# Conv-attention and a four-block Mamba on one core: group norm's matmuls, statistics loads, input order and the last fusion rescheduled

## The chip, the core and the metric

The kernel runs on one core of a Trainium2 chip. A core has five engines that run side by side, each working through its own queue in order: TensorE (PE in the profile, its weight loads PEld), VectorE (DVE), ScalarE (ACT), GpSimd (POOL) and SyncE (SP), which here only issues DMAs. The metric is the device time of one execution in microseconds (us). Before the change it is 8983.23 us, the median of three runs (8980.16 to 8992.36).

## The reference

The input is x, of shape 8 x 512 x 48 x 48 in fp32: 8 samples of 512 channels and 2304 positions. Two layers follow each other, each with a group norm in front and a residual around it.

```python
x = x + _L0_conv_ref(_gn(x), L0_conv_Wq, ...)    # causal linear attention
x = x + _L1_conv_ref(_gn(x), L1_conv_in_proj_w, ...)
```

Layer 0 projects to q, k and v (8 heads of 64), applies elu + 1 to q and k, and computes causal linear attention over the positions: a running sum of k times v, read by q and divided by q times the running sum of k.

Layer 1 splits the channels into 4 blocks of 128. Block i takes its own channels plus the fused output of block i - 1, and runs a Mamba over the positions: an input projection, a causal convolution of 4 taps, silu, a projection to dt, B and C, softplus, a state recurrence of 16 states for each of 256 inner channels, a gate and an output projection. Then it fuses:

```python
fused_global = jnp.maximum(x_i, x_m)
w_local = jax.nn.sigmoid(jnp.mean(x_i, axis=(2, 3), keepdims=True))
w_global = jax.nn.sigmoid(jnp.mean(fused_global, axis=(2, 3), keepdims=True))
return w_local * x_i + w_global * fused_global
```

The group norm has 32 groups of 16 channels and takes mean and variance over a group's channels and all positions.

## The kernel before

Positions are cut into 6 chunks of 384 (LC). The recurrence is the bulk of the work: a job is one chunk of one block of one sample, 192 jobs in all, each of 8 slots. A slot does four scans on VectorE (`scan`, L844), each with a decay factor from ScalarE's exp into a PSUM bank (`decay`, L833), the product of B and the input partly on VectorE (`product`, L823) and partly on GpSimd (`last_product`, L812), a product with C on GpSimd (`weigh`, L860), and a gather on TensorE that adds the states up (`gather`, L867). Two streams of jobs (even samples, odd samples) alternate by a fixed pattern; the last job is stream 1's.

All other work is written as generators ("tasks") that a planner steps at two places in each slot, `beside(2k)` before the scans of slot k and `beside(2k + 1)` after two of them. These are called halves. A generator yields when its next stage is due and how many PSUM banks the stage needs: a tuple `(half, gap)` means not before that half and at least `gap` halves after its last stage; a string such as `"1"` means that many halves after its last stage. A stage whose banks are not spare is put off, and so are stages behind it that need banks. There are 6 such banks; three usually hold decays. The engines run what is issued in the order of issue, so the planner's order is every queue's order.

The tasks are these. `chunk(m)` is one attention chunk for one block of 128 channels; its stages are due at `times[m] + j`, and its end copies the new x from PSUM (L463), takes statistics of it (bn_stats, L467), and after the sixth chunk runs `group_norm` for that block's input of layer 1. `group_norm` (L162) has five stages, whose places its caller can give: aggregate the statistics and a first matmul that averages over groups (L171), subtract (L174 to L178), a second matmul (L186), add epsilon and a power on GpSimd (L188, L191), and the factors (L195). `statistics(b)` takes the statistics of a whole sample for layer 0's group norm: for samples above 0 it loads 24 pieces, one each 16 halves (`PERIOD`), and runs bn_stats on each (L239); for sample 0 it loads x in six large DMAs (L219). `weights()` loads a block's weights for a stream (L493 to L510) and scales the convolution's on GpSimd (L516). `pass_on()` fuses the block that has ended and writes the input of the next one, `xi`, chunk by chunk: ScalarE scales the maximum `fu` and `xi` (L610, L611), GpSimd adds them (L618), and the new `xi` is either the sum with the normalized x (L623, blocks 1 to 3), or, when a new sample starts (`fresh`), the normalized x alone, written by ScalarE (L621); it may overwrite `xi` only after the add at L618 has read it. GpSimd then adds the residual (L626), and the result is stored. `self.ready` tells the planner that a job may begin. `prepare()` of a job makes its convolution (L649) and the rest, due at fixed halves ahead of the job's first slot. Its softplus writes `delta` (L720) and frees two banks late.

`save` and `flush` put off stores by a few halves; SP issues loads and stores in the planner's order.

Of the kernel before, what the change touches and what calls it, by code (L numbers as in the profile page):

```python
# [9 lines left out]
F32 = mybir.dt.float32  # L10
AF = mybir.ActivationFunctionType
ALU = mybir.AluOpType
# [4 lines left out]
P = 128  # L17
T = 128
LC = 384
# [30 lines left out]
def attention_then_mamba_kernel(  # L50
# [17 lines left out]
    nc = tc.nc  # L68
    B, _, L = x.shape
    NS = 16  # L70
    NC = L // LC
# [5 lines left out]
    mpool = ctx.enter_context(tc.tile_pool(name="mamba", bufs=2))  # L77
# [21 lines left out]
    def load_projections(o):  # L99

        src = wqkv.rearrange("(t p) c -> p t c", p=P)
        for j in range(3):
            cols = slice(j * 512 + o * P, j * 512 + (o + 1) * P)
            nc.sync.dma_start(out=wq_sb[:, :, cols], in_=src[:, :, cols])
# [49 lines left out]
    def save(out, in_):  # L154
        stores.append((half_no[0], out, in_))

    def flush(every=True):
        while stores and (every or stores[0][0] <= half_no[0] - 2):
            _, o, i = stores.pop(0)
            nc.sync.dma_start(out=o, in_=i)  # L160
# [46 lines left out]
    norms, xns, x1s, done, ksums = {}, {}, {}, {}, {}  # L207

    def statistics(b):

        xv = x[b].rearrange("(t p) l -> p t l", p=P)
        stats = small.tile([P, 4, NC, 6], F32, tag="stats_a", name=f"stats_a{b}", bufs=2)
        if b == 0:

            xs = []

            def load(c):
                t = mpool.tile([P, 4, 1 + LC], F32, tag="u", name=f"xs_{c}", bufs=5)[:, :, 0:LC]
                nc.sync.dma_start(out=t, in_=xv[:, :, c * LC : (c + 1) * LC])  # L219
                xs.append(t)  # L220

            for c in range(5):
                load(c)
            load_projections(0)
            for c in range(NC):
                for ct in range(4):
                    nc.vector.bn_stats(stats[:, ct, c, :], xs[c][:, ct, :])
                if c == 0:
                    load(5)
                    fetch(0)  # L230
            for o in range(1, 4):
                load_projections(o)
        else:
            when = begins[b] + b % 2
            for i in range(4 * NC):
                yield (when - 2, 1) if b > 1 else "1", 0
                xs = piece(b, i)
                yield (when, 1) if b > 1 else "1", 0
                nc.vector.bn_stats(stats[:, i // NC, i % NC, :], xs)  # L239
                when += PERIOD  # L240
        norms[b] = yield from group_norm(stats, 4, f"a{b}", 2)

    def piece(b, i):
        ct, c = i // NC, i % NC
        xs = apool.tile([P, LC], F32, tag="xs", name=f"xs_{b}_{i}", bufs=2)
        nc.sync.dma_start(out=xs, in_=x[b][ct * P : (ct + 1) * P, c * LC : (c + 1) * LC])
        return xs
# [3 lines left out]
    def fetch(m):  # L251

        if m == len(parts):
            return
        b, o, c = parts[m]
        if (o, c) == (0, 0):
            xns[b] = dpool.tile([512, L], F32, tag="xn", name=f"xn_{b}", bufs=B)
            x1s[b] = dpool.tile([512, L], F32, tag="x1", name=f"x1_{b}", bufs=B)
        xn = apool.tile([P, 4, LC], F32, tag="xn", name=f"xn_{b}_{o}_{c}", bufs=2)
        src = (x[b] if o == 0 else xns[b]).rearrange("(t p) l -> p t l", p=P)  # L260
        nc.sync.dma_start(out=xn, in_=src[:, :, c * LC : (c + 1) * LC])
        fetched[m] = xn
# [3 lines left out]
    def chunk(m):  # L266


        b, o, c = parts[m]
# [3 lines left out]
        cols, tile_rows = slice(c * LC, (c + 1) * LC), slice(o * P, (o + 1) * P)  # L273
# [58 lines left out]
        S, stats, ksum = passes[b, o]  # L332
# [107 lines left out]
        for i in range(NT):  # L440
            old = c > 0 or i > 0
# [25 lines left out]
        nc.vector.bn_stats(stats[:, 0, c, :], xr)  # L467
        if c + 1 == NC:
            norm = yield from group_norm(
                stats, 1, f"m{b}_{o}", 8, [(times[m] + j, 1) for j in (28, 29, 29, 30, 32)]  # L470
            )
            flush()
            done[b, o] = norm

    class Stream:
# [62 lines left out]
        def pass_on(self):  # L538


            xi = self.xi
            old = None
            if self.b is not None:
                old = self.b, self.s, self.n, self.fm
                wt = small.tile([P, 4], F32, tag="wt", name=f"wt_{self.n}")
                nc.vector.tensor_copy(wt[:, 2:3], self.sums)
                nc.vector.tensor_reduce(wt[:, 3:4], self.fsum, AX.X, ALU.add)
            last = old is not None and old[1] == 3 and not self.samples
# [29 lines left out]
            def loads(c):  # L578
                fu = xb = xa = None
                cols = slice(c * LC, (c + 1) * LC)  # L580
                if not last:
                    xb = mpool.tile([P, LC], F32, tag="xb", name=f"xb_{self.n}_{c}")
                    nc.sync.dma_start(out=xb, in_=x1s[self.b][s * P : (s + 1) * P, cols])
                if old is not None:
                    fu = mpool.tile([P, LC], F32, tag="fu", name=f"fu_{old[2]}_{c}")
                    nc.sync.dma_start(out=fu, in_=old[3][:, cols])
                    xa = mpool.tile([P, LC], F32, tag="xo", name=f"xo_{old[2]}_{c}")
                    nc.sync.dma_start(out=xa, in_=x1s[old[0]][old[1] * P : (old[1] + 1) * P, cols])
                return fu, xb, xa

            now = loads(0)
            for c in range(NC):

                if c and not last:
                    first = 2 * self.jobs[self.block * NC + c].start
                    yield (first - 33, 1), 0
                    now = loads(c)
                    yield (first - 25, 1), 0
                elif c:
                    yield "3", 0  # L600
                    now = loads(c)
                    yield "1", 0
                else:
                    yield "1", 0
                cols, icols = slice(c * LC, (c + 1) * LC), slice(3 + c * LC, 3 + (c + 1) * LC)
                fu, xb, xa = now
                if not last:
                    normed = dict(bias=norm[:, 1, :], scale=norm[:, 0, :])
                if old is not None:
                    nc.scalar.activation(fu, fu, AF.Copy, scale=wt[:, 1:2])  # L610
                    nc.scalar.activation(xi[:, icols], xi[:, icols], AF.Copy, scale=wt[:, 0:1])  # L611
                if old is None:
                    nc.scalar.activation(xi[:, icols], xb, AF.Identity, **normed)
                elif not last and not self.fresh:
                    nc.scalar.activation(xb, xb, AF.Identity, **normed)
                if old is not None:
                    yield "1", 0
                    nc.gpsimd.tensor_tensor(fu, fu, xi[:, icols], ALU.add)  # L618
                    yield "1", 0
                    if not last and self.fresh:  # L620
                        nc.scalar.activation(xi[:, icols], xb, AF.Identity, **normed)  # L621
                    elif not last:
                        nc.gpsimd.tensor_tensor(xi[:, icols], xb, fu, ALU.add)  # L623
                    self.ready = c + 1
                    yield "1", 0
                    nc.gpsimd.tensor_tensor(xa, xa, fu, ALU.add)  # L626
                    save(out[old[0], old[1] * P : (old[1] + 1) * P, cols], xa)
                self.ready = c + 1
# [331 lines left out]
    def first_scan(b, o):  # L960
        own = [j.start for j in jobs if j.stream is streams[b % 2]]
        return own[(b // 2 * 4 + o) * NC]

    parts, times = [], []
    for b, o in sorted(((b, o) for b in range(B) for o in range(4)), key=lambda t: first_scan(*t)):
        for c in range(NC):
            when = 2 * first_scan(b, o) - BEFORE - (NC - 1 - c) * PERIOD
# [75 lines left out]
    def at(k):  # L1043
        return jobs[k // SLOTS], k % SLOTS
# [31 lines left out]
    def prime(k):  # L1076
        job, s = at(k)
        hurry(k, lambda: job.prepared)
        primed.add(k)
        job.inputs(0)  # L1080
        for r in range(2):
            us[k + r] = job.last_product(s + r)
        job.product(s, us[k])
        ahead(DEPTH)
# [48 lines left out]

    with tc.manual_schedule():
        half_no[0] = FIRST - 6
        for st in streams:
            tasks.append(Task(st.weights()))
            tasks.append(Task(st.pass_on()))
        Task(statistics(0)).finish()
        for half in range(FIRST - 6, 0):  # L1140
            beside(half)
        prime(0)
        for k in range(slots):
            slot(k)
# [70 lines left out]
```

## Time and profile before

| | us |
|---|---|
| median of three runs | 8983.23 |
| profiled execution | 8983.06 |
| its span (first to last instruction) | 8981.0 |
| VectorE busy in it | 8252.1 |
| GpSimd busy | 8058.8 |
| TensorE busy | 7759.3 |
| ScalarE busy | 6629.5 |

The profile is of one execution. Its span is divided into busy and idle time for each engine; for idle time it names what ended it, the instruction or DMA whose completion the engine waited for. Busy TensorE time is modelled, as matmuls are pipelined. The five costliest groups of instructions (line, engine, operation, shapes and count | busy us, mean ns of one | idle time of the engine just before them, and what ended it):

```profile
L844 DVE TENSOR_TENSOR_SCAN u<-bank,u 128x385 f32<-128x385 f32 (+1 forms) x6144 | 5449.4, 937 | 273.8 <-ACT bank L833 253.5
L860 POOL TENSOR_TENSOR u<-u,C 128x1536 f32<-128x1536 f32 x1536 | 4880.9, 3178 | 142.8 <-DVE u L844 36.1
L833 ACT ACTIVATE bank<-dr,av 128x385 f32<-128x385 f32 (+1 forms) x6144 | 3418.0, 578 | 995.0 <-DVE u L844 768.6
L867 PE MATMUL yp<-u,cst 128*64 128x384 f32 x12288 | 2471.0, 524 | 389.7 <-POOL u L860 313.1
L812 POOL TENSOR_TENSOR u<-B,dxr 128x512 f32<-128x512 f32 x1536 | 1958.9, 1275 | 19.6 <-DMA dxr<-xscr 17.5
```

### The profile page before, as it was taken

What the parts mean: (1) busy time and instruction counts of PE and PEld (TensorE: products, weight loads), DVE (VectorE), ACT (ScalarE), POOL (GpSimd) and SP (SyncE); (2) the same over time, 40 slices, a digit from 0 to 9 for tenths busy, and PEclk for the clock granted to TensorE, in tenths of its full rate; (3) what the DMA queues carried; (4) which work ended last, traced back from release to release, by engine and by line L of the source; (5) the groups of instructions that cost most, each with busy time, mean ns of one, the idle gap of its engine ahead of it and who ended that gap; (6) DMA issues with size and microseconds to landing.
All of it is one profiled execution on the core that took longest, in us unless ns stands there. A gap on an engine that the chain in (4) does not pass through costs nothing.

```text
span 8981.0 us, 121595 instructions
## 1 busy us (share of the span) xinstructions
PE 7759.3 (86%) x36098; PEld 3681.5 (41%) x36098; DVE 8252.1 (92%) x11448; ACT 6629.5 (74%) x12848; POOL 8058.8 (90%) x5635
## 2 busy tenths in 40 slices
PE   7888888888888889888888888898888888888864
PEld 4444444443444444443344444444444444444321
DVE  3999999998899999999999999999989999999997
ACT  2777777777777777777777777777777777777775
POOL 1888999999999899999998999998999999999998
PEclk9999999999999999999999999999999999999987
DMA  6666776666666677676666667676666676666654
GB/s 189 163 176 180 192 190 189 187 186 186 188 181 180 182 192 193 188 185 189 188 187 184 182 187 191 191 192 182 189 188 187 182 187 181 182 181 179 173 156 131
DMA packets 1002901, 1642.89 MB, mean 183 GB/s; under 512 B 138593, under 2 KB 797313, under 8 KB 1002241
## 3 DMA queue, kind: packets, MB, share of 16 engines
q1 hardware_dynamic: 1002240, 1635.13, 67.2%
q8 instruction: 287, 4.70, 0.2%
q14 instruction: 374, 3.06, 0.1%
HBM read 1309.06 MB, written 325.58 MB: 182 GB/s over the span
## 4 chain that ended last, share of the span: by engine, by line
DVE 37%; POOL 13%; PE 13%; ACT 13%; DMA 11%; issue 8%; SPq 4%; POOLq 0%; DVEq 0%; ACTq 0%
DVE u L844 23%; POOL u L860 8%; DVE u L823 7%; ACT bank L833 4%; PE bank L286 4%; PE yp L867 3%; SPq L753 3%; PE bank L649 3%; DMA C<-scr 2%; POOL u L812 2%; ACT L833 2%; ACT L720 2%; DMA dscr<-delta 1%; DVE yz L879 1%; DMA xo<-x 1%
## 5 line engine op out<-in xcount | busy, mean ns | idle before, releaser
L844 DVE TENSOR_TENSOR_SCAN u<-bank,u 128x385 f32<-128x385 f32 (+1 forms) x6144 | 5449.4, 937 | 273.8 <-ACT bank L833 253.5
L860 POOL TENSOR_TENSOR u<-u,C 128x1536 f32<-128x1536 f32 x1536 | 4880.9, 3178 | 142.8 <-DVE u L844 36.1
L833 ACT ACTIVATE bank<-dr,av 128x385 f32<-128x385 f32 (+1 forms) x6144 | 3418.0, 578 | 995.0 <-DVE u L844 768.6
L867 PE MATMUL yp<-u,cst 128*64 128x384 f32 x12288 | 2471.0, 524 | 389.7 <-POOL u L860 313.1
L812 POOL TENSOR_TENSOR u<-B,dxr 128x512 f32<-128x512 f32 x1536 | 1958.9, 1275 | 19.6 <-DMA dxr<-xscr 17.5
L823 DVE TENSOR_TENSOR u<-B,dxp 128x1024 f32<-128x1024 f32 x1536 | 1833.1, 1193 | 10.6 <-ACT dxp L796 10.6
L286 PE MATMUL bank<-xn,wq_sb 128*128 128x384 f32 x4608 | 1681.1, 508 | 88.3 <-POOL xn L310 33.2
L867 PEld LDWEIGHTS yp<-u,cst 128*64 128x64 f32 x12288 | 788.5, 141 | 1615.6 <-issue 865.7
L649 PE MATMUL bank<-xi,wk 128*128 128x384 f32 x3072 | 1104.1, 502 | 274.3 <-ACT kl L383 184.1
L286 PEld LDWEIGHTS bank<-xn,wq_sb 128*128 128x128 f32 x4608 | 854.1, 196 | 833.9 <-DVE k L351 137.7
L649 PEld LDWEIGHTS bank<-xi,wk 128*128 128x128 f32 x3072 | 556.0, 191 | 834.0 <-ACT kl L383 290.8
L298 ACT ACTIVATE ex<-bank,bqkv_sb 128x384 f32<-128x384 f32 x384 | 221.3, 576 | 639.3 <-PE bank L286 639.2
L761 POOL TENSOR_TENSOR delta<-delta,xs 128x384 f32<-128x384 f32 x384 | 384.3, 1001 | 255.8 <-DMA dscr<-delta 191.0
L858 POOL COPY state<-u 128x4 f32<-128x4 f32 x1280 | 242.0, 189 | 334.9 <-DVE u L844 329.0
L833 ACT ACT_TABLE_LOAD x382 | 490.1, 1283 | 6.8
L801 ACT ACTIVATE yp<-xs,pv 128x384 f32<-128x384 f32 x384 | 223.9, 583 | 316.7 <-DVE yz L879 316.5
L709 PE MATMUL bank<-dbc,wd 9*128 9x384 f32 x768 | 316.9, 534 | 1.3 <-ACT dbc L701 1.3
L885 PE MATMUL bank<-yz,wo 128*128 128x384 f32 x768 | 295.6, 506 | 16.3 <-DVE yz L879 14.2
L660 PE MATMUL bank<-xi,wi 128*128 128x384 f32 x768 | 287.4, 496 | 13.1 <-ACT xs L685 13.1
L696 PE MATMUL bank<-xs,wx 128*40 128x384 f32 x768 | 281.0, 488 | 0.8 <-DVE sm L434 0.8
L453 PE MATMUL bank<-sm,v 128*64 128x128 f32 x2304 | 257.6, 302 | 0.0
L416 PE MATMUL bank<-cst,rdb 128*128 128x128 f32 x576 | 120.1, 325 | 150.7 <-DVE u L844 148.7
(111 smaller groups left out, 7902.5 us busy)
## 6 DMA issues: line engine op xcount, KB each, us to landing
B<-scr SPq DMA_DIRECT2D x1536, 192.0 KB
C<-scr SPq DMA_DIRECT2D x1536, 192.0 KB
xn<-xn SPq DMA_DIRECT2D x192, 768.0 KB
dr<-dscr SPq DMA_DIRECT2D x768, 192.0 KB
dxr<-xscr SPq DMA_DIRECT2D x768, 192.0 KB
dscr<-delta SPq DMA_DIRECT2D x192, 384.0 KB
xscr<-delta SPq DMA_DIRECT2D x192, 384.0 KB
xn<-in_x SPq DMA_DIRECT2D x48, 768.0 KB
```

The lines of the kernel that those rows point to most:

```text
L286: nc.tensor.matmul(ps, wq_sb[:, kt, j * 512 + o * P : j * 512 + (o + 1) * P], xn[:, kt, :], start=(kt == 0), stop=(kt == 3),)
L649: nc.tensor.matmul(xc, wk[:, k, h * P : (h + 1) * P], xi[:, c0 + k : c0 + k + LC], start=(k == 0), stop=(k == 3),)
L660: nc.tensor.matmul(zp, wi[:, 256 + h * P : 256 + (h + 1) * P], xi[:, c0 + 3 : c0 + 3 + LC], start=True, stop=True,)
L709: nc.tensor.matmul(vp, wd[32:41, h * P : (h + 1) * P], dbc[32:41, :], start=True, stop=True)
L761: nc.gpsimd.tensor_tensor(delta[:, h, :], delta[:, h, :], xs[:, h, :], ALU.mult)
L812: nc.gpsimd.tensor_tensor(u[:, :, :, 1 + LC - TAIL :], self.B[s % 4][:, :, cols].unsqueeze(2).to_broadcast(shape), self.dxr[s // 4][:, :, ...
L823: nc.vector.tensor_mul(u[:, :, :, 1 : 1 + LC - TAIL], self.B[s % 4][:, :, cols].unsqueeze(2).to_broadcast(shape), self.dxp.unsqueeze(1).to ...
L833: nc.scalar.activation(dA[:, cols], self.dr[h][:, g, cols], AF.Exp, scale=self.w[6][:, 2 * h + g, q + j : q + j + 1],)
L844: nc.vector.tensor_tensor_scan(u[:, j, g, cols], dA[:, cols], u[:, j, g, cols], 0.0, ALU.mult, ALU.add,)
L860: nc.gpsimd.tensor_tensor(h, h, self.C[s % 4].unsqueeze(2).to_broadcast([P, NG, 2, LC]), ALU.mult)
L867: nc.tensor.matmul(self.yp[g * 64 : g * 64 + 64, 0:LC], pair_sum, u[:, j, g, 1:], start=False, stop=(s % 4 == 3 and j == NG - 1), skip_gro ...
L885: nc.tensor.matmul(self.xm[:, 0:LC], self.w[2][:, h, :], self.yz[:, h, :], start=(h == 0), stop=(h == 1),)
```

## The change

Five edits. The group norm of layer 1 gets new places: its first stage with the bn_stats in front of it, its second matmul with the subtraction. A sample's statistics pieces are loaded four halves before their bn_stats rather than two. A fresh input chunk after the first is written two halves after the add rather than one. Sample 0's statistics, with their loads, are issued before the weights and streams are set up. And the last fusion of stream 1, which has no block after it, is written anew: it loads everything at once into three of the large `u` buffers and does the two multiply-adds of each chunk on VectorE.

```diff
             for i in range(4 * NC):
-                yield (when - 2, 1) if b > 1 else "1", 0
+                yield (when - 4, 1) if b > 1 else "1", 0
                 xs = piece(b, i)
...
             norm = yield from group_norm(
-                stats, 1, f"m{b}_{o}", 8, [(times[m] + j, 1) for j in (28, 29, 29, 30, 32)]
+                stats, 1, f"m{b}_{o}", 8, [at(28, 0), at(29), at(29, 0), at(30), at(32)]
             )
...
+            if last and self.z:
+
+                got = [
+                    mpool.tile([P, 4, 1 + LC], F32, tag="u", name=f"end_{i}", bufs=5)
+                    for i in range(NC // 2)
+                ]
+                for c in range(NC):
+                    fu, xa = (got[c // 2][:, c % 2 * 2 + i, 0:LC] for i in range(2))
+                    cols = slice(c * LC, (c + 1) * LC)
+                    rows = slice(old[1] * P, (old[1] + 1) * P)
+                    nc.sync.dma_start(out=xa, in_=x1s[old[0]][rows, cols])
+                    nc.sync.dma_start(out=fu, in_=old[3][:, cols])
+                for c in range(NC):
+                    fu, xa = (got[c // 2][:, c % 2 * 2 + i, 0:LC] for i in range(2))
+                    cols, icols = slice(c * LC, (c + 1) * LC), slice(3 + c * LC, 3 + (c + 1) * LC)
+                    for t, i in ((xi[:, icols], 0), (fu, 1)):
+                        nc.vector.scalar_tensor_tensor(
+                            xa, t, wt[:, i : i + 1], xa, ALU.mult, ALU.add
+                        )
+                    nc.sync.dma_start(out=out[old[0], rows, cols], in_=xa)
+                return
             now = loads(0)
...
                     nc.gpsimd.tensor_tensor(fu, fu, xi[:, icols], ALU.add)
-                    yield "1", 0
+                    yield "2" if c and self.fresh and not last else "1", 0
                     if not last and self.fresh:
                         nc.scalar.activation(xi[:, icols], xb, AF.Identity, **normed)
...
         half_no[0] = FIRST - 6
+        Task(statistics(0)).finish()
         for st in streams:
             tasks.append(Task(st.weights()))
             tasks.append(Task(st.pass_on()))
-        Task(statistics(0)).finish()
```

`at(j, gap)` stands for `(times[m] + j, gap)`, with a gap of 1 where none is given.

## The prediction

> **What bounds the kernel now.** First the page, then the waits by engine, then timelines at the places where the change acts.
>
> ```profile
> PE 7759.3 (86%) x36098; PEld 3681.5 (41%) x36098; DVE 8252.1 (92%) x11448; ACT 6629.5 (74%) x12848; POOL 8058.8 (90%) x5635
> ...
> DVE u L844 <- ACT bank L833: 253.5, 187, 4.6
> DVE q L343 <- ACT bank L299: 145.5, 66, 6.0
> DVE stats_a L239 <- DMA xs<-in_x: 54.2, 34, 3.7
> ...
> DVE gm_m L188 <- PE bank L186: 11.0, 31, 1.3
> ...
> DVE norm_m L195 <- POOL norm_m L191: 8.0, 7, 2.1
> ...
> ACT xi L621 <- POOL fu L618: 110.5, 36, 9.2
> ...
> PEld bank L186 <- ACT delta L720: 127.3, 30, 4.3
> ```
>
> VectorE (DVE) is the pacing engine: 8252.1 of 8981.0 us, with GpSimd (POOL) close behind. Everything the program does is one stream of slots, 1536 of them, so a slot costs some 5.8 us and a half slot (the planner's clock) 2.9 us. The chain of waits runs through all engines and settles little, so I price each edit by the DVE idle time that it can remove. The waits (us in total, times, longest) add up to about 664 us of DVE idle; some 150 us lie in the first 250 us, where the first sample is prepared and no scan runs yet.
>
> One group norm of the 32 shows what its matmuls do (columns: start, us, instruction, and in brackets the idle time before it):
>
> ```profile
> 1126.66 0.55 DVE L467 BATCH_NORM_STATS2 stats_m<-xr 128x6 f32<-128x384 f32 x1
> ...
> 1130.05 0.29 DVE L169 BATCH_NORM_AGGREGATE mv_m<-stats_m 128x2 f32<-128x36 f32 x1
> ...
> 1137.05 0.87 ACT L720 ACTIVATE delta<-bank 128x384 f32<-128x384 f32 x2
> 1137.59 0.50 PEld L186 LDWEIGHTS bank<-gm_m,cst 128*128 128x128 f32 x2 [4.27 <-ACT delta L720]
> ...
> 1138.11 2.83 PE L867 MATMUL yp<-u,cst 128*64 128x384 f32 x8
> ...
> 1141.56 3.75 PE L286 MATMUL bank<-xn,wq_sb 128*128 128x384 f32 x8
> ...
> 1146.40 0.55 DVE L343 SCALAR_TENSOR_TENSOR q<-ex,bank 128x384 f32<-128x384 f32 x1 [2.33 <-ACT bank L299]
> ```
>
> The second matmul (L186) takes a PSUM bank that the softplus L720 has still to read, so TensorE stands 4.27 us; the next gathers and projection come late, ScalarE's exp with them, and DVE loses 2.33 us at `q`.
>
> The end of the run is a bare chain; one chunk of six:
>
> ```profile
> 8959.26 0.34 SPq L160 DMA_DIRECT2D out<-xo  x1
> 8959.65 0.42 SPq L586 DMA_DIRECT2D fu<-fm  x1
> 8960.12 0.44 SPq L588 DMA_DIRECT2D xo<-x  x1
> 8962.19 0.61 ACT L610 ACTIVATE fu<-fu,wt 128x384 f32<-128x384 f32 x1 [5.09 <-DMA fu<-fm]
> 8962.71 0.60 ACT L611 ACTIVATE xi<-xi,wt 128x384 f32<-128x384 f32 x1
> 8963.38 0.99 POOL L618 TENSOR_TENSOR fu<-fu,xi 128x384 f32<-128x384 f32 x1 [4.15 <-ACT xi L611]
> 8964.45 0.99 POOL L626 TENSOR_TENSOR xo<-xo,fu 128x384 f32<-128x384 f32 x1
> ```
>
> Nothing else runs, and each chunk's loads are issued only behind the store of the one before: 6.2 us a chunk.
>
> **What the Trainium skill says.** "TensorE: Matmul & The Clock Gate", Part 1, has the array fall to half its clock after an idle window of about 3.4 us. The trace agrees: after 4.27 us of idling the eight gathers take 2.83 us, elsewhere (1126.65) 1.51, so a stall costs more than its own length. "GPSIMD Engine Reference", 4.1, gives two-input elementwise work to VectorE, GPSIMD being about 2x slower; here an add of 128x384 takes 0.99 on POOL and a two-operation DVE instruction of that size 0.55 (L343). "DMA: Bandwidth & Descriptors", "Issuing engines are not separate DMA queues", says that all transfers share 16 DMA engines; at the start that decides what reordering can win.
>
> **Part 1, group norm's matmuls sooner.** Gaps decide the real halves. Before, counted from bn_stats at half 28: aggregate and first matmul 29, subtraction 30, second matmul 31, add and power 32, factors 33. After: 28, 29, 29, 30, 32. The second matmul thus leaves the softplus's half (31) and is two halves ahead of it. Its bank is then the one that the subtraction has just freed on DVE, so it waits for DVE alone. What is queued behind it on PE (gathers, L709) waits with it: from the timeline DVE would finish the subtraction near 1130.85, PE would reach the matmul near 1131.1, so 0 to 0.3 us. The first matmul stands behind L696 (until 1129.4) and DVE has the aggregate done near 1128.0: no wait. DVE's own instructions stay the same. POOL's power moves two halves forward, into a place where POOL waited 0.50 us for DVE, so `norm_m` no longer waits for it. DVE idle that goes: 27 of the waits at `q` stand 7.6 to 9.1 us behind such a stall and sum to 51.3; L188 9.0 at the same places; L195 6.6. Together 66.9; I leave 7 for new waits at the subtraction (0.2 x 32). Gain in DVE idle 60. Banks: at half 28 three decays, the x-projection, the next chunk's denominators and now the first matmul need 6 of 6 banks; it just fits.
>
> **Part 2, statistics loaded two halves (5.8 us) earlier.** In steady state 17 of the 144 pieces find DVE waiting, 0.37 to 3.04 us, 24.8 in sum (the rest of the 54.2 is sample 1 at the start, unchanged). All are shorter than 5.8, so all go; two buffers suffice, since the piece before is read 12 halves earlier. SP issues the same DMA once, 0.43 us. Gain 25.
>
> **Part 3, fresh input a half later.** ScalarE stops at L621 for GpSimd's fusion add; 30 of the 36 stops (c > 0) are moved. DVE feels only the long ones, four waits a pair of streams: 1.70, 4.58, 1.06 and 4.16, so 11.5, three times over 34.5. A half more lets two decays and their scans through; stops of 8.5 and 7.1 us outlast it, and I leave 1.8 and 1.4. Gain 25. POOL's later add and its store slip a half, beside other work. The convolution that reads the input follows one half later, so PE may wait there; it reached it some 5 us after L621 in the worst case (2455.5 to 2460.7).
>
> **Part 4, x ahead of weights.** SP issues x at 12.26 now, behind 18 weight DMAs; then at 1.64, so first statistics, norm and normalized chunk come 10.6 us sooner. But the weights (10 us of SP) move behind the projections and ahead of sample 1's pieces and the second chunk's input, which start at 35.72 now and about 33 to 35 then; DMA is saturated until 44 us (share 1.06 to 1.22 in the windows from 16), and ScalarE's exp of `av` stands in its queue ahead of the first feature exp (41.97 now, about 38 then). The first chunks hang on those transfers: gain 3, from 0 to 8.
>
> **Part 5, last fusion on VectorE.** From L561's end (8941.35) to the span's end are 39.7 us. After: SP issues 12 loads at some 0.47 each from 8940.9, the last near 8946.5, landing 2.1 later, 8948.6. DVE needs 12 x 0.55 = 6.6 from about 8944, so it ends near 8950.7; then an issue and landing as now (8978.02 to 8981.0, 3.0): 8953.7. Gain 27, from 24 to 29; nothing stands beside it, so it is all on the path.
>
> **Sum.** DVE idle of parts 1 to 3 doesn't convert wholly, since POOL is at 90% and comes late at other places: I take 0.8, 0.8 and 0.7 (POOL itself is what is late in part 3), so 48 + 20 + 17 = 85. With 3 and 27: 115. The profiled execution took 8983.06 (span 8981.0 and 2.1 around it), 0.2 under the median 8983.23: 8868.
>
> **Rivals.**
> Half gains: GpSimd takes DVE's place. Its 8058.8 us leave less room than DVE's idle suggests, and it is busy without a break from 1135 to 1146. If a quarter of 110 converts: 27 + 3 + 27 = 57, 8926. Against it: POOL's waits for DVE (L858, 329.0) show that it mostly follows DVE.
> Full gains: every wait becomes time, the start gives 8: 67 + 25 + 34 + 8 + 27 = 161, 8822.
> Slower: the sixth bank. If at half 28 one more bank is held, the planner puts off the stages that need one, the x-projection's chain or the denominators, by a half, 2.9 us for each of 32 blocks, with nothing won in part 1: 32 x 2.9 = 93 against 27 + 3 + 20 + 17 = 67, so 9009. It decides once a group norm costs DVE 2.7 us more than it does today ((67 + 18) / 32). For it: the count above leaves no bank. Against it: banks are freed by both DVE and ScalarE steps ahead of the second matmul.
> The change does less than it says: the stall merely moves with the matmuls, parts 2 to 5 small: near 8970.
>
> **How the numbers follow.** Forecast 0.64, half gains 0.20, full gains 0.06, slower 0.06, hardly anything 0.04. Range 8825 to 8935: it takes in the bounds of the parts (60 to 160 gained) and most of the half-gain case. Against 0.2% (18 us, about what can be told from no change here), all but the last two cases are faster: 0.90, same 0.04, slower 0.06.
>
> **What would show it.** L186's wait for L720 gone and no gathers of 2.8 us behind it; `q` L343's waits near 95 instead of 145.5; `stats_a` waits only before 100 us; L621's 110.5 reduced to some 40; first bn_stats near 6 us but the first scan only some 3 us earlier; after L561 less than 14 us to the end. It is wrong if new waits of DVE for PE at L174 or for POOL at L844 eat the gain, or if the first matmul's half shows PE standing for DVE.

## The result, and the profile after

| | before | after |
|---|---|---|
| median, us | 8982.74 (8980.16 to 8992.36, 4 runs) | 8895.12 (8893.49 to 8897.16, 4 runs) |
| profiled execution, us | 8983.06 | 8897.16 |
| its span | 8981.0 | 8895.4 |
| start of the first scan | 225.6 | 230.8 |
| start of the last scan | 8932.4 | 8872.9 |
| from the last scan to the end of the span | 48.5 | 22.5 |

The change takes about 88 us: the ratio is 0.9901, 95% interval 0.9883 to 0.9918. Of the 85.6 us between the two spans, 26.0 come from the tail and 64.8 from the stretch with scans; the start gives 5.3 back. From L591 on the lines of the kernel after are numbered 21 higher: the scan is L865, the decay's exp L854, the add of the fusion L639, the write of a fresh input L642.

The page and the waits by engine of the kernel after (engine, instruction and line, what it waited for: us in total, times, longest):

```profile
PE 7715.9 (87%) x36098; PEld 3655.0 (41%) x36098; DVE 8248.8 (93%) x11460; ACT 6631.2 (75%) x12836; POOL 8054.4 (91%) x5623
...
DVE u L865 <- ACT bank L854: 267.2, 209, 4.1
DVE q L343 <- ACT bank L299: 97.0, 52, 6.0
...
ACT xi L642 <- POOL fu L639: 81.7, 36, 7.8
...
PE bank L186 <- ACT delta L741: 1.8, 1, 1.8
...
POOL delta L782 <- DMA dscr<-delta: 248.1, 100, 22.4
```

VectorE, ScalarE and GpSimd are busy as long as before, so the gain is idle time. VectorE's wait at `q` fell from 145.5 to 97.0, and the second matmul's wait for the softplus (108.8 before, and 127.3 on its weight loads) is down to one of 1.8. But the wait of VectorE for decays (L865) rose from 253.5 to 267.2, and GpSimd's wait for `dscr`, the spread of `delta` through memory, from 191.0 to 248.1.

The timeline of the kernel after at the group norm that the prediction shows (start, us, instruction, in brackets the idle time before it):

```profile
1126.32 0.55 DVE L467 BATCH_NORM_STATS2 stats_m<-xr 128x6 f32<-128x384 f32 x1
...
1129.71 0.13 DVE L174 COPY gm_m<-bank 128x1 f32<-128x1 f32 x1
1130.52 0.38 PE L186 MATMUL bank<-gm_m,cst 128*128 128x1 f32 x2
...
1130.83 1.51 PE L888 MATMUL yp<-u,cst 128*64 128x384 f32 x8
```

The second matmul runs at 1130.52 with no idle time before it, and the gathers behind it take 1.51 us, not 2.83. That part works as forecast. The gain is not spread evenly, though. Comparing the starts of the same scans in both traces:

| scan | 0 | 1280 | 1536 | 2560 | 3072 | 4096 | 4608 | 5888 |
|---|---|---|---|---|---|---|---|---|
| after minus before, us | +5.3 | -7.1 | -5.6 | -35.2 | -30.0 | -44.5 | -37.3 | -59.8 |

From 1280 to 1536, 2560 to 3072 and 4096 to 4608, where the streams change to new samples, the kernel after is slower, by 1.6, 5.2 and 7.2 us; it gains in the other stretches of the table. The forecast has nothing that loses there. The order of SyncE's queue has. Before, at a group norm of such a stretch (SPq are DMA issues):

```profile
4149.26 1.25 SPq L740 DMA_DIRECT2D dr<-dscr  x2
4150.60 0.54 SPq L261 DMA_DIRECT2D xn<-in_x  x1
4157.39 0.38 SPq L160 DMA_DIRECT2D xn<-xn  x1
...
4159.82 0.55 SPq L729 DMA_DIRECT2D dscr<-delta  x1
...
4164.55 1.01 POOL L761 TENSOR_TENSOR delta<-delta,xs 128x384 f32<-128x384 f32 x1 [0.81 <-DMA dscr<-delta]
```

After, at the same one:

```profile
4117.47 0.38 SPq L160 DMA_DIRECT2D xn<-xn  x1
4117.90 1.99 SPq L761 DMA_DIRECT2D dr<-dscr  x2
4119.99 0.57 SPq L261 DMA_DIRECT2D xn<-in_x  x1
...
4121.90 0.53 SPq L750 DMA_DIRECT2D dscr<-delta  x1
...
4129.61 1.00 POOL L782 TENSOR_TENSOR delta<-delta,xs 128x384 f32<-128x384 f32 x1 [6.31 <-DMA dscr<-delta]
```

`chunk` calls `flush()` right after its group norm (L472). The last place was half 33 in fact and is 32 now, so `flush()` comes a half sooner, and with it the store `xn<-xn`, whose data GpSimd normalizes (L310). The store waits for GpSimd at the head of SyncE's queue, 9.8 us here and 6.2 before. The spread `dscr` stands behind it in both kernels. What changed places are the loads of `dr` and `xn`: they used to be ahead of the store and stand behind it now. So the DMA engines move nothing from 4111 to 4117, where before they were busy at a share of 0.91 to 0.96 (4151 to 4155, after these loads were issued), and the loads then go out directly ahead of the spread. The spread is issued 1.4 us before GpSimd is free for it, in place of 3.9, and GpSimd goes on 7.7 us after that issue, in place of 4.7. GpSimd loses 6.31 us on `dscr` where it lost 0.81. This place occurs six times in the run. The first theory therefore reads: the new places are worth more than 57 us, and their last one gives a part of it back through `flush()`.

### The profile page after: what moved, and what is told of

Its sections match the earlier page's. It is cut to its first block, busy times and chain, and to the rows that moved or that the text cites. A ratio compares the mean times of both kernels' runs of the same rounds, so it can differ in the third digit from the quotient of the medians.

```text
span 8895.4 us, 121686 instructions
## 1 busy us (share of the span) xinstructions
PE 7715.9 (87%) x36098; PEld 3655.0 (41%) x36098; DVE 8248.8 (93%) x11460; ACT 6631.2 (75%) x12836; POOL 8054.4 (91%) x5623
## 4 chain that ended last, share of the span: by engine, by line
DVE 41%; POOL 13%; PE 13%; ACT 12%; DMA 10%; issue 8%; SPq 4%; POOLq 0%; DVEq 0%; ACTq 0%
DVE u L865 26%; DVE u L844 8%; POOL u L881 7%; ACT bank L854 4%; PE bank L670 4%; PE bank L286 3%; SPq L774 3%; POOL u L833 2%; PE yp L888 2%; ACT L854 2%; DMA C<-scr 2%; DMA dscr<-delta 1%; PE bank L681 1%; ACT L741 1%; DVE yz L900 1%
## 5 line engine op out<-in xcount | busy, mean ns | idle before, releaser
L865 DVE TENSOR_TENSOR_SCAN u<-bank,u 128x385 f32<-128x385 f32 (+1 forms) x6144 | 5456.0, 939 | 302.9 <-ACT bank L854 267.2
L854 ACT ACTIVATE bank<-dr,av 128x385 f32<-128x385 f32 (+1 forms) x6144 | 3422.4, 578 | 1018.3 <-DVE u L865 804.7
L888 PE MATMUL yp<-u,cst 128*64 128x384 f32 x12288 | 2434.4, 518 | 438.5 <-POOL u L881 365.6
L782 POOL TENSOR_TENSOR delta<-delta,xs 128x384 f32<-128x384 f32 x384 | 385.1, 1003 | 288.1 <-DMA dscr<-delta 248.1
```

The costliest lines, as they stand in the source:

```text
L782: nc.gpsimd.tensor_tensor(delta[:, h, :], delta[:, h, :], xs[:, h, :], ALU.mult)
L854: nc.scalar.activation(dA[:, cols], self.dr[h][:, g, cols], AF.Exp, scale=self.w[6][:, 2 * h + g, q + j : q + j + 1],)
L865: nc.vector.tensor_tensor_scan(u[:, j, g, cols], dA[:, cols], u[:, j, g, cols], 0.0, ALU.mult, ALU.add,)
L888: nc.tensor.matmul(self.yp[g * 64 : g * 64 + 64, 0:LC], pair_sum, u[:, j, g, 1:], start=False, stop=(s % 4 == 3 and j == NG - 1), skip_gro ...
```

## The experiments

Every kernel was timed beside the kernel before on the same chip; the ratios are to it. Differences between two of these kernels are from medians unless ratios are given.

### Parts of the change alone, and the last place

`p1_norm_alone` is the kernel before with the new places only, `p1_norm_33` the same with the last place where it had been:

```diff
-                stats, 1, f"m{b}_{o}", 8, [(times[m] + j, 1) for j in (28, 29, 29, 30, 32)]
+                stats, 1, f"m{b}_{o}", 8, [at(28, 0), at(29), at(29, 0), at(30), at(32)]   # p1_norm_alone
+                stats, 1, f"m{b}_{o}", 8, [at(28, 0), at(29), at(29, 0), at(30), at(33)]   # p1_norm_33
```

> The kernel before with the group norm's new places and nothing else. Theory A (the forecast's part 1): the stalls at the second matmul go and nothing takes their place, 48 us less. Theory B (flush): a group norm ends with a flush of all stores put off so far, and it now ends a half sooner; at six group norms, two at each change of sample, this puts the store of a normalized chunk (which waits for GpSimd) ahead of the loads and of the spread of delta in SyncE's queue, so that GpSimd and then VectorE wait: about 30 us are given back there, 15 to 30 us less in all, and the stretches at a change of sample are no faster than before.

> The same with the last of the five places at 33 in place of 32, so that factors and flush stay in the half where they were; both matmuls are still moved. Theory A: as the run with 32, within 3 us. Theory B: SyncE's order is that of before at those six places, GpSimd's long waits for the spread of delta there go, and it is 20 to 35 us faster than with 32, 45 to 55 us under before.

Measured: 8924.89 us (ratio 0.9942, 0.993 to 0.9955) and 8899.6 us (0.9911, 0.9897 to 0.9924), against 8982.01 before. The new places are worth 82 us, and the last one gives 25 of them back. Scans 2560 to 3072 took 746.7 us before, 752.0 with the last place at 32 and 742.8 with it at 33, so the difference shows where the theory puts it. That difference, 25, is what theory B gave; in size both runs beat it (57 and 82 us against 15 to 30 and 45 to 55). The waits of `p1_norm_alone`:

```profile
POOL delta L761 <- DMA dscr<-delta: 262.2, 103, 22.0
```

and of `p1_norm_33`:

```profile
POOL delta L761 <- DMA dscr<-delta: 229.3, 107, 25.1
```

GpSimd waits 33 us less for `dscr` when `flush()` keeps its place. At the six places it stands some 5 us longer each with 32, 30 in sum; nowhere else do the two runs differ by more than 3.2 us. At the first of the six both are alike up to the store (issued at 1945.50 with 32, 1945.49 with 33), and GpSimd is free for the spread at 1951.32 and 1951.31. But the spread is issued at 1949.90 and 1947.92, and GpSimd goes on at 1957.34 and 1952.47: of 4.9 us, 2.0 are the later issue, and in the other 2.9 the spread is on its way. The expectation has the store moved ahead of the spread as well; it was moved ahead of the loads only. The last place moves the norm's factors along with `flush()`; that the 25 us are the flush's rests on these six places.

The other parts, each alone on the kernel before (`p2_stats_alone`, `p3_fresh_alone`, `p4_start_alone`, `p5_tail_alone`; each takes its lines of the change's diff and nothing else):

> The kernel before with the statistics' pieces loaded four halves ahead and nothing else. Forecast: the 17 waits of 24.8 us after the first 250 us go and 20 us of it become time. Rival: the waits only stood in other engines' shadow, under 8 us.

> The kernel before with the fresh input a half later and nothing else. Forecast: VectorE's waits behind the moved step shrink from 34.5 to about 10 us and 17 us less in all. Rival: GpSimd is what is late there, and the same time is lost at its products: under 6 us less.

> The kernel before with sample 0's statistics ahead of the weights and nothing else. Forecast: first scan 3 us sooner, 3 us less in all. Theory T (transfers only change places): first statistics 8 to 10 us sooner, but sample 1's first piece and the second chunk's input are issued 2 us later than now, since the weights stand in front of them; first scan 0 to 5 us later, time the same within 5 us.

> Kernel before plus the last fusion on VectorE alone. Forecast: 27 us less (24 to 29), so 8956; the stretch from the last scan to the end falls from 48.5 to 22 to 24 us, and nothing else changes.

| alone | forecast, us | median, us | before, us | ratio, interval |
|---|---|---|---|---|
| statistics loads | -20 | 8978.44 | 8982.01 | 0.9997, 0.9989 to 1.0005 |
| fresh input | -17 | 8981.1 | 8982.01 | 0.9998, 0.999 to 1.0006 |
| start | -3 | 8980.06 | 8982.01 | 1.0003, 0.9994 to 1.0011 |
| last fusion | -27 | 8955.39 | 8978.14 | 0.9974, 0.9963 to 0.9985 |

The last fusion does what was forecast in its place: from the last scan to the end it takes 22.3 us instead of 48.5. The medians differ by 22.8, a little under the 24 to 29 expected, which the interval (13 to 33) takes in. The other three do nothing that can be told, although two of them take waits away. The intervals leave no room for the 20 and the 17; the 3 of the start are too few to be told from nothing. VectorE's waits with the statistics loads alone:

```profile
DVE u L844 <- ACT bank L833: 267.4, 202, 4.6
DVE q L343 <- ACT bank L299: 148.2, 69, 6.7
DVE yz L879 <- PE yp L867: 45.7, 30, 5.7
...
DVE stats_a L239 <- DMA xs<-in_x: 28.9, 16, 3.7
```

`stats_a` fell by 25.3, and what is left lies at the start; the three rows above it rose by 13.9, 2.7 and 3.4. All idle time of VectorE adds up to 689.2 us before and 689.0 here. At one place, before:

```profile
1618.38 0.56 DVE L239 BATCH_NORM_STATS2 stats_a<-xs 128x6 f32<-128x384 f32 x1 [3.04 <-DMA xs<-in_x]
```

and between the same scans with the statistics loaded earlier, where the piece's bn_stats ran at 1625.27 without a wait:

```profile
1626.43 1.81 DVE L844 TENSOR_TENSOR_SCAN u<-bank,u 128x385 f32<-128x385 f32 x2 [0.61 <-POOL u L812]
1631.63 2.66 DVE L844 TENSOR_TENSOR_SCAN u<-bank,u 128x385 f32<-128x385 f32 x3 [0.50 <-ACT bank L833]
```

Of the 3.04 us, 1.11 come back within some 6 us, as waits for GpSimd and ScalarE. A few scans farther on (1638.78 before, 1646.35 here) the run has still gained 2.5 us on the kernel before. Where that is lost again, the trace doesn't say.

The fresh input alone shows the same: VectorE's idle time is 687.7 us. ScalarE's stops at L621 fall from 110.5 to 64.2 us and VectorE's wait for decays from 253.5 to 240.2, but its wait at `q` rises from 145.5 to 152.4 and the time stays.

### The start, in the whole kernel

`a_norm_33` is the kernel after with the last place at 33. `a33_old_start` undoes the start in it. `a33_late_weights` keeps x first and moves weights behind what the first chunk needs:

```diff
         Task(statistics(0)).finish()
-        for st in streams:
-            tasks.append(Task(st.weights()))
-            tasks.append(Task(st.pass_on()))
+        tasks.append(Task(streams[0].weights()))
+        tasks.append(Task(streams[0].pass_on()))
+        def late():      # stream 1, due at half -106
+            yield -106, 0
+            tasks.append(Task(streams[1].weights()))
+            tasks.append(Task(streams[1].pass_on()))
+        def rest():      # projections of blocks 1 to 3, at halves -70, -50, -30
+            for o in range(1, 4):
+                yield -90 + 20 * o, 0
+                load_projections(o)
+        tasks.append(Task(late()))
+        tasks.append(Task(rest()))
```

> The changed kernel with the last place at 33 in place of 32 and nothing else. Theory B (flush): the store of the normalized chunk goes back behind the spread of delta in SyncE's queue at six group norms, and as in the pair on the kernel before this is worth 20 to 30 us: 8865 to 8875. Rival (the other edits already cover it): under 8 us.

> The run with 33, with the weights ahead of sample 0's statistics again. Theory T: within 5 us of it. If the 5 us by which the changed kernel's first scan came late were the start's doing: 5 us less than it.

> The run with 33, with less standing in front of sample 1: after sample 0's statistics only stream 0's weights are issued, stream 1's 12 halves later, and the projections of the other three blocks from half -70, 20 halves apart. Theory T: 6 to 7 us of SyncE's issues and some 3 MB go from in front of sample 1's pieces and the second chunk's input, which are issued near 26 us in place of 38: first scan 6 to 10 us sooner, 6 to 10 us less. Rival (the start hangs on the chunks' own chain of TensorE, ScalarE and VectorE steps): under 3 us.

Measured: 8877.62 (0.9883, 0.9868 to 0.9898), 8876.48 (0.9883, 0.987 to 0.9897) and 8867.1 us (0.9873, 0.986 to 0.9887). The place at 33 takes 17.5 us off the kernel after by the medians, somewhat less than expected. All its four runs (up to 8880.88) are faster than all four of the kernel after (from 8893.49), though the two ratios' intervals overlap. Nothing can be told of the start edit, and the timeline shows why. SyncE's queue in the kernel after:

```profile
1.64 5.25 SPq L219 DMA_DIRECT2D xs<-in_x  x5
...
36.82 0.42 SPq L510 DMA_DIRECT2D av<-in_alog  x1
...
38.13 0.33 SPq L246 DMA_DIRECT2D xs<-in_x  x1
38.50 0.43 SPq L261 DMA_DIRECT2D xn<-in_x  x1
```

x is issued first, but then the weights of both streams stand ahead of sample 1's pieces and of the second chunk's input. Before, those were issued at 35.72 and 36.60; now at 38.13 and 38.50, 2 us later. With the weights late they go out at 24.66 and 25.03, as expected, and the first scan starts at 227.6 rather than 236.1, but first scans differ by several us between runs with no edit at the start at all (225.1 and 230.3 in `p3_fresh_alone` and `p5_tail_alone`), and the ratios' intervals overlap. That this order gains some 10 us is likely, not settled.

### What is late for the spread

Of GpSimd's waits those for `dscr` grew most with the change, and there are many outside the changes of sample. The timeline of the kernel after at an ordinary end of a block:

```profile
5398.37 0.59 SPq L493 DMA_DIRECT2D wi<-in_win  x1
...
5399.71 0.42 SPq L500 DMA_DIRECT2D wo<-in_wout  x1
5403.39 0.33 SPq L502 DMA_DIRECT2D wx<-in_wxp  x1
...
5406.27 0.43 SPq L510 DMA_DIRECT2D av<-in_alog  x1
5407.92 0.38 SPq L750 DMA_DIRECT2D dscr<-delta  x1
...
5410.85 1.00 POOL L782 TENSOR_TENSOR delta<-delta,xs 128x384 f32<-128x384 f32 x1 [6.89 <-DMA dscr<-delta]
...
5415.28 2.71 PE L888 MATMUL yp<-u,cst 128*64 128x384 f32 x8 [3.91 <-POOL u L881]
```

The nine weight loads of the stream's next block are issued from 5398.37 to 5406.70, ahead of the spread, which GpSimd needs at 5403.96. GpSimd stands 6.89 us; TensorE, waiting for GpSimd, stands 3.91 and then does the gathers in 2.71. Issuing the nine takes 3.7 us of the 8.3; in most of the rest SyncE stands for transfers to land. SyncE's longest waits from 5398 to 5409:

```profile
SPq L502 <- DMA xn<-xn: 3.2, 1, 3.2
SPq L750 <- DMA wk<-in_wconv: 0.8, 1, 0.8
```

The 7676 DMAs that SyncE issues in this program take eight semaphores in turn, and in the trace none is issued before the DMA eight places ahead of it, which had the same semaphore, has landed. So `wx` waits for a load of `xn` issued at 5395.26, and the spread itself for the weight load `wk` of 5399.01. So the theory for part 3's small worth and for the long GpSimd waits is one and the same, and it can be tried by exchanging two neighbours:

```diff
-            if c == NC - 1 and (st.s < 3 or st.samples):
-                tasks.append(Task(st.weights()))
...
             dsrc = spread("dscr")
+            if c == NC - 1 and (st.s < 3 or st.samples):
+                tasks.append(Task(st.weights()))
```

`b_weights_after` is `a33_late_weights` with it; `b_weights_after_no3` also undoes the fresh input; `b_no23` is `a33_late_weights` with fresh input and statistics loads undone.

> a33_late_weights, and the next block's weights (nine loads) are asked for after the spread of dscr at a block's last chunk, instead of ahead of it in SyncE's queue. Theory (GpSimd, coming late at block ends because its dscr arrives late, is what is still late in part 3's place): GpSimd's waits for dscr at L782 fall from some 230 to 250 us to about 100, ScalarE's long stops at L642 shrink, and the time falls by 15 to 40 us from 8867, to 8830 to 8850. Rival (that lateness lies in shadow, since GpSimd waits for VectorE elsewhere): the waits fall but the time stays within 6 us of 8867, the idle time going to GpSimd's waits for VectorE at L879.

> b_weights_after with part 3 undone (fresh input one half after the add, as before). If GpSimd's lateness caused the stops at L642, part 3 is now worth nothing: within 5 us of b_weights_after. By the forecast's reading part 3 is worth 17: 17 us more than b_weights_after.

> a33_late_weights with parts 2 and 3 both undone. Forecast's reading: 20 + 17 = 37 us more than 8867, so 8904. Theory from the runs of each alone (waits taken away here come back at the next dependence): within 6 us of 8867. Rival (they are worth something once the group norm is out of the way): 10 to 25 us more.

| | median, us | ratio to before, interval |
|---|---|---|
| `a33_late_weights` | 8867.1 | 0.9873, 0.986 to 0.9887 |
| `b_weights_after` | 8770.15 (8760.7 to 8771.46) | 0.9765, 0.9752 to 0.9779 |
| `b_weights_after_no3` | 8765.46 (8759.23 to 8772.41) | 0.9763, 0.975 to 0.9776 |
| `b_no23` | 8870.16 | 0.9881, 0.9867 to 0.9894 |

The exchange takes 97 us, more than the whole change gave and more than twice what was expected. The same place in `b_weights_after`, whose lines are numbered 2 or 3 lower:

```profile
5324.01 0.52 SPq L745 DMA_DIRECT2D dscr<-delta  x1
5324.62 0.41 SPq L491 DMA_DIRECT2D wi<-in_win  x1
...
5330.61 1.00 POOL L779 TENSOR_TENSOR delta<-delta,xs 128x384 f32<-128x384 f32 x1
```

The weights follow the spread, and GpSimd no longer stands. The waits of `a33_late_weights`:

```profile
DVE q L341 <- ACT bank L297: 105.2, 52, 6.0
DVE yz L898 <- PE yp L886: 32.5, 23, 4.9
...
POOL state L877 <- DVE u L863: 243.4, 211, 14.1
POOL delta L780 <- DMA dscr<-delta: 198.5, 94, 23.5
...
ACT xi L640 <- POOL fu L637: 70.3, 35, 8.2
```

and of `b_weights_after`:

```profile
DVE q L341 <- ACT bank L297: 76.7, 35, 6.0
DVE yz L897 <- PE yp L885: 10.2, 6, 4.9
...
POOL state L876 <- DVE u L862: 256.6, 217, 13.5
POOL delta L779 <- DMA dscr<-delta: 115.1, 95, 23.5
...
ACT xi L640 <- POOL fu L637: 36.6, 36, 3.1
```

GpSimd's wait for `dscr` falls by 83.4 us. This row holds only what the profile puts down to the spread: at the 30 ends of blocks all idle time of GpSimd ahead of the spread's first use falls from 151.1 to 20.7 us, and the spread is issued 1.8 us after the softplus on average, not 9.8. VectorE's idle time falls by 86.0 (599.5 to 513.5), 50.8 of it in the two rows shown, and the span by 90.3. 30 blocks load weights for a following one, so each gives some 3.0 us. The rival expected the idle time to move to GpSimd's wait for VectorE (`state`); that rose by only 13.2.

Without part 3 the same kernel takes as long (0.9763 against 0.9765), although ScalarE's stops at L640 sum to 87.3 us then, 50.7 more. Those stops cost nothing here. They had cost nothing in the kernel before either, where GpSimd was late, so this pair doesn't show that GpSimd's lateness was what made part 3 worthless. And without parts 2 and 3 the time is within 3 us by medians and 7 by ratios, where the forecast's terms ask for 37.

## Why the prediction held, and where its working failed

The forecast was 8868, 115 us less; 88 were measured. The direction and the two parts that carry the gain were right. The sum was nearer than its terms deserve.

- **Part 1.** Mechanism right: L186's wait is gone, the gathers behind it run in 1.51 us, no new wait of VectorE for the first matmul appeared (L174: 0.7 us before, 0.5 after), and the sixth bank put nothing off: in `p1_norm_33` every engine has all its other instructions in the order of before. One of the forecast's signs of being wrong showed in small: the scans' waits for GpSimd rose from 19.8 to 35.2. The term was 48 (60 of idle time by 0.8). The new places alone give 82: VectorE's idle time falls by 80 (689 to 609) and the time with it, one to one, so both the 60 and the factor 0.8 were too small. The wait at `q` alone fell by 61 where I counted 51, more than the 27 stops that I had assigned to the stall.
- **The step that failed.** I moved the group norm's own instructions and priced them, but not what its caller issues when it returns: `flush()` at L472. It came a half sooner with the last place and put a store that waits for GpSimd ahead of two loads, which then went out together with the spread of `dscr` and delayed it. That cost 25 us alone (17.5 in the whole). That leaves 57 of the 82, by chance close to my 48.
- **Part 2 (20) and part 3 (17).** Both waits go as forecast: no `stats_a` wait is left behind the start, and L621's stops shrink. Neither gives time. The factors of 0.8 and 0.7 on idle time were the error: what VectorE no longer waited for here it waited for elsewhere, for ScalarE, GpSimd or TensorE, and its idle time in sum stayed. L642 ended at 81.7 rather than my 40, partly because `flush()` made GpSimd late there: with the last place at 33 it is 66.2.
- **Part 4 (3).** Nothing that can be told. I saw that the weights move ahead of sample 1's pieces and still put those at 33 to 35; they came at 38.13. The first statistics start at 8.35 us, not 6, so 8.6 sooner and not 10.6, and the first scan is not sooner.
- **Part 5 (27).** Right: 26 in the tail. After L561's end come 13.6 us, against 12.35 worked out, mainly since each of the twelve fused instructions takes 0.62 and not the 0.55 of L343.

By measured terms: 82 - 25 + 0 + 0 + 26 = 83, against 88. The rival of half gains had the right thought, that GpSimd leaves less room than VectorE's idle time suggests, but a quarter for everything is as wrong as 0.8 for everything: part 1 converted wholly, parts 2 and 3 not at all. What sets them apart is argued, not shown: the stall at L186 held up the gathers, and the late spread held up GpSimd, and with them what feeds the next slot; the waits of part 2 stood at VectorE alone, and part 3 let ScalarE go on sooner but made no engine that it waited for earlier.

What stays open is where the remaining part of a removed wait comes back.

## What to carry to other kernels

Before pricing a wait that goes, find who else is late at that place: L186's stall of TensorE was worth all the idle time that it caused at VectorE, while VectorE's waits for loads and ScalarE's for the fusion's add were worth nothing, and their sizes alone didn't say so. When a stage is moved, list everything that is issued on its return, stores and flushes included, and look at what stands behind each in its queue: behind a store that waited for its data the loads stood still here, and the DMA engines ran empty for 6 us. And read the DMA queue at places where a nearly full engine waits for a small transfer: here the neighbour ahead of it was worth more than all five edits.

## What the runs showed of the hardware that was not expected

A small transfer can be late by its place in the queue more than by its own way. Once issued, the spread of 5407.92 let GpSimd go on 2.9 us later (5410.85); nine weight loads, of 0.24 to 0.65 us each in SyncE's queue, with the stops between them, had held it back by 9.5 us (5398.37 to 5407.92). The Trainium skill ("DMA: Bandwidth & Descriptors", "Issuing engines are not separate DMA queues") calls the time that a sequencer takes to initiate a DMA "usually small relative to the DMA itself". For one DMA the trace agrees (0.38 us for the spread). But nine ahead of one add up to 3.7 us, and the stops for the landing of DMAs eight places ahead to 5.0 more (3.2, 0.8, 0.8 and 0.2), and the order was worth 97 us.

The reduced clock of TensorE showed again without L186: after 3.91 us of waiting for GpSimd the eight gathers took 2.71 us, at a granted clock of 0.53, elsewhere 1.51. "TensorE: Matmul & The Clock Gate", Part 1, names idle windows of about 3.4 us for it. The trace agrees in part: in the kernel after, 21 of the 22 groups of gathers that followed at least 3.4 us of idling took more than 2 us, but so did 26 of the 45 that followed 2.0 to 3.4 us, so the slow gathers are seen after shorter stalls as well. With the spread ahead of the weights the mean granted clock rose from 0.967 (`a33_late_weights`) to 0.974.
